# A state space scan: two VectorE operations a step on y alone, the chunks' own part summed by TensorE, the gate by one Silu

## The chip, the cores and the metric

The kernel runs on one core of a Trainium2 chip. The metric is the device time in microseconds (us) of one execution. Engines by the names of the profile: PE is TensorE, DVE is VectorE, ACT is ScalarE, POOL is GpSimd, SP is SyncE, which here only issues DMAs. PEld is TensorE's weight load, which overlaps its matmuls.

## The reference, cut to what matters

The program is a chain of two layers on one sequence of 2048 tokens with 128 channels: a state space mixer, a layer of experts, a causal attention, and then six blocks of windowed attention and feed-forward. The change is in the first of these, the state space mixer:

```python
A = relu(A_diag); dt = sigmoid(dt_p)
Bu = einsum('bth,phc->btpc', x, B_param)          # 128 states p, real and imaginary c
S = 1.0 / (1.0 + dt * dt * A)
m11, m12, m21, m22 = S, -dt * A * S, dt * S, S
f1, f2 = dt * S, dt * dt * S
def step(carry, bu):                              # 2048 steps
    z, y = carry
    z1 = c(m11) * z + c(m12) * y + c(f1) * bu
    y1 = c(m21) * z + c(m22) * y + c(f2) * bu
    return (z1, y1), y1
o = einsum(ys[..., 0], C_param[..., 0]) - einsum(ys[..., 1], C_param[..., 1]) + x * D
g = hidden @ Wg.T
o = o * rsqrt(mean(o * o) + EPS) * norm_weight * (g * sigmoid(g))
return o @ Wo.T
```

Here x is the normed input times Wi. From the two equations y alone obeys y[t] = 2 S y[t-1] - S y[t-2] + dt dt S bu[t], a recurrence of second order with no z in it. (The first equation gives dt z1 = y1 - y.)

## The kernel before, in words

The state lies with its 128 states p on the partitions. The 2048 steps are cut into 128 chunks of CL = 16 steps; the chunks lie side by side in the free dimension, so that one operation advances all of them, real and imaginary part, by one step: 128 partitions by 2 x 128 elements. The work of the front part has four stages.

- **Inputs** (ssm_step, ssm_inputs, lines 213 to 289): the step's coefficients; then for each of four groups of 512 tokens the layer norm ("ln_st", "ln_r", "ln_h", "ln_pt", "hT"; "ln_r" is a power on POOL), x by Wi ("px", kept as xsT), the two inputs Bu ("pb") scaled by dt S into f1 (laid out step, part, chunk), ACT for the real and DVE for the imaginary part, and the gate's product ("pg"). ACT makes Sigmoid of "pg" into sg and copies "pg" into the gate (a view of x3T); POOL multiplies the two.
- **Scan** (ssm_scan, lines 291 to 335), all on DVE: first the chunks' own recurrence, three operations a step (t from y, z from z and t, y from z), with ys and f1 as views of the tile kT; then the states at the chunks' ends go through seven doubling rounds of four operations each (the log scan, in zy, a view of hT3), with powers of the step's 2x2 matrix that POOL makes beside it (ssm_powers); then, for each of the 16 steps, two operations add what the state carried into the chunk contributes. The result yo is in token order.
- **Output** (ssm_out, lines 337 to 372): for each group "po" sums y by C and x by D on PE, DVE multiplies by the gate ("ou"), ACT makes the squares' sums ("osq"), PE transposes ("pu"), POOL makes the inverse root ("or_"), PE multiplies by Wo ("pr"), DVE adds to x.
- **Experts, keys and values, attention** follow ("own", "py", "pl", "pk", "pv").

Each engine runs its instructions in the order in which the program writes them (InOrder, line 56). From the output stage on that order comes from Merge (line 71): each group's work is a generator that yields a waiting time, and the pieces are written in the order of their due times. The times at which the groups begin stand in front (line 529): output of group 0 at 0, of 2 at 7, of 1 at 10, of 3 at 16; experts of group 0 at 9, of 1 at 22, of 2 at 41, of 3 at 57; keys and values from 43 on. These are numbers that set an order, not times. PSUM gives seven banks to all tiles of these stages.

Between the inputs and the scan, front puts on POOL: a memset of zy's left half, the powers, the products diag_d, ct, w_igo and bqk, two iotas, the split of two bias rows into three bf16 pieces (split_rows, with two DMAs on SP), and a memset of va (128 x 8192 elements), the attention's values. One tile pool ("s1") gives the scratch tiles; its tiles have two buffers where nothing else is said, zt among them.

Of the kernel before, what the change touches and what calls it, by code (L numbers as in the profile page):

```python
# [11 lines left out]
F32 = mybir.dt.float32  # L12
BF16 = mybir.dt.bfloat16
I32 = mybir.dt.int32
AF = mybir.ActivationFunctionType
ALU = mybir.AluOpType
# [3 lines left out]
P = 128  # L20
T = 2048
NT = T // P
G = 4
NG = NT // G
# [7 lines left out]
HD1 = P // HEADS1  # L32
# [13 lines left out]
CL = 16  # L46
NCH = T // CL
PAD = NCH // 2
# [45 lines left out]
class Kernel:  # L94
# [117 lines left out]

    def ssm_step(self, w):

        vec, dve = self.w1[1], self.dve
        am = w.tile([P, 1], F32, name="am")
        dve.tensor_scalar_max(am, vec[:, 0:1], 0.0)
        dt = w.tile([P, 1], F32, name="dt")
        self.act.activation(dt, vec[:, 1:2], AF.Sigmoid)
        dta = w.tile([P, 1], F32, name="dta")  # L220
        dve.tensor_tensor(dta, dt, am, ALU.mult)
        den = w.tile([P, 1], F32, name="den")
        dve.tensor_scalar(den, dta, dt, 1.0, ALU.mult, ALU.add)
        npow = int(math.log2(T // 2)) + 1
        pw = w.tile([P, npow, 4], F32, name="pw")
        dve.reciprocal(pw[:, 0, 0:1], den)
        dve.tensor_copy(pw[:, 0, 3:4], pw[:, 0, 0:1])
        dve.tensor_scalar(pw[:, 0, 1:2], dta, pw[:, 0, 0:1], -1.0, ALU.mult, ALU.mult)
        dve.tensor_scalar_mul(pw[:, 0, 2:3], dt, pw[:, 0, 0:1])
        return dt, pw  # L230

    def ssm_powers(self, w, pw):

# [21 lines left out]
            n, k = 2 * n, k + 1  # L255
        return rows

    def ssm_inputs(self, pool, psum, x, g, m21, f1, gate, xsT):

        w4, vec, bt, ct = self.w1  # L260
        cpg = GW // CL
        hT = pool.tile([P, GW], F32, name="hT", tag="t")
        yield from self.norm_transposed(pool, psum, x, g, hT)
        px = psum.tile([P, GW], F32, name="px", tag="b")
        self.pe.matmul(px, lhsT=w4[:, 0, :], rhs=hT, start=True, stop=True)
        xs_g = xsT[:, g * GW : (g + 1) * GW]
        self.dve.tensor_copy(xs_g, px)
        yield 3.0
        for c in range(2):
            pb = psum.tile([P, GW], F32, name="pb", tag="b")  # L270
            self.pe.matmul(pb, lhsT=bt[:, c, :], rhs=xs_g, start=True, stop=True)
            fg = f1[:, :, c, g * cpg : (g + 1) * cpg].rearrange("p l k -> p k l")
            pb = pb.rearrange("p (k l) -> p k l", l=CL)
            if c == 0:
                self.act.activation(fg, pb, AF.Copy, scale=m21)
            else:
                self.dve.tensor_scalar_mul(fg, pb, m21)
        yield 14.0
        pg = psum.tile([P, G, P], F32, name="pg", tag="b")
        for j in range(G):  # L280
            self.pe.matmul(
                pg[:, j, :], lhsT=hT[:, j * P : (j + 1) * P], rhs=w4[:, 1, :], start=True, stop=True
            )
        yield 3.0
        sg = pool.tile([P, G, P], F32, name="sg", tag="t")
        self.act.activation(sg, pg, AF.Sigmoid)
        gg = gate[:, g * G : (g + 1) * G, :]
        self.act.copy(gg, pg)
        self.gps.tensor_tensor(gg, gg, sg, ALU.mult)

    def ssm_scan(self, pool, dt, pw, rows, f1, ys, zy, yo):

        dve = self.dve
        s_, m12 = pw[:, 0, 0:1], pw[:, 0, 1:2]

        zp, yp = zy[:, 0:2], zy[:, 2:4]
        z = f1[:, 0]
        dve.tensor_scalar_mul(ys[:, 0], z, dt)
        for l in range(1, CL):
            t = pool.tile([P, 2, NCH], F32, name="zt")  # L300
            dve.scalar_tensor_tensor(t, ys[:, l - 1], m12, f1[:, l], ALU.mult, ALU.add)
            zn = pool.tile([P, 2, NCH], F32, name="zn") if l < CL - 1 else zp[:, 0, :, PAD:]
            dve.scalar_tensor_tensor(zn, z, s_, t, ALU.mult, ALU.add)
            dve.scalar_tensor_tensor(ys[:, l], zn, dt, ys[:, l - 1], ALU.mult, ALU.add)
            z = zn
        dve.tensor_copy(yp[:, 0, :, PAD:], ys[:, CL - 1])

        cur, step, k = 0, 1, int(math.log2(CL))
        while step < NCH:
            zc, yc, zn, yn = zp[:, cur], yp[:, cur], zp[:, 1 - cur], yp[:, 1 - cur]  # L310
            lo, hi = PAD - step, PAD + NCH - step
            ts = []
            for row, old in enumerate((zc, yc)):
                ts.append(pool.tile([P, 2, NCH], F32, name="zt"))
                dve.scalar_tensor_tensor(
                    ts[row], zc[:, :, lo:hi], pw[:, k, 2 * row : 2 * row + 1], old[:, :, PAD:],
                    ALU.mult, ALU.add,
                )
            for row, new in enumerate((zn, yn)):
                dve.scalar_tensor_tensor(  # L320
                    new[:, :, PAD:], yc[:, :, lo:hi], pw[:, k, 2 * row + 1 : 2 * row + 2], ts[row],
                    ALU.mult, ALU.add,
                )
            cur, step, k = 1 - cur, 2 * step, k + 1
        cz = zp[:, cur, :, PAD - 1 : PAD - 1 + NCH]
        cy = yp[:, cur, :, PAD - 1 : PAD - 1 + NCH]
        for l in range(CL):
            t = pool.tile([P, 2, NCH], F32, name="zt")
            dve.scalar_tensor_tensor(
                t, cz, rows[:, 0, l : l + 1], ys[:, l], ALU.mult, ALU.add  # L330
            )
            dve.scalar_tensor_tensor(
                yo.rearrange("p c (k l) -> p c k l", l=CL)[:, :, :, l], cy, rows[:, 1, l : l + 1], t,
                ALU.mult, ALU.add,
            )

    def ssm_out(self, pool, psum, x, g, gate, xsT, yo):

        w4, ct, diag_d = self.w1[0], self.w1[3], self.diag_d
        po = psum.tile([P, G, P], F32, name="po", tag="b")  # L340
        for j in range(G):
            cols = bass.ts(g * G + j, P)
            self.pe.matmul(po[:, j, :], lhsT=yo[:, 0, cols], rhs=ct[:, 0, :], start=True, stop=False)
            self.pe.matmul(po[:, j, :], lhsT=yo[:, 1, cols], rhs=ct[:, 1, :], start=False, stop=False)
            self.pe.matmul(po[:, j, :], lhsT=xsT[:, cols], rhs=diag_d, start=False, stop=True)
        yield 3.2
        u = pool.tile([P, G, P], F32, name="ou", tag="t")
        self.dve.tensor_tensor(u, po, gate[:, g * G : (g + 1) * G, :], ALU.mult)
        sq = pool.tile([P, G, P], F32, name="osq", tag="t")
# [126 lines left out]
    def front(self, ctx, merge, psum, kvpool, x, hT3, kT, va, xsT):  # L476


        nc, tc, gps = self.nc, self.tc, self.gps
# [13 lines left out]
        gate = self.x3T.rearrange("p (n c) -> p n c", c=P)  # L493
# [5 lines left out]
        zy = hT3[:, 0 : 8 * (PAD + NCH)].rearrange("p (a c k) -> p a c k", c=2, k=PAD + NCH)  # L499
        half = CL * 2 * NCH  # L500
        kf = kT.rearrange("p n t -> p (n t)")
        f1 = kf[:, 0:half].rearrange("p (l c k) -> p l c k", c=2, k=NCH)
        yo = kf[:, 0:half].rearrange("p (c t) -> p c t", c=2)
        ys = kf[:, half:].rearrange("p (l c k) -> p l c k", c=2, k=NCH)

        dt, pw = self.ssm_step(self.w1pool)
        first = Merge()
        for g in range(NG):
            first.add(2.5 * g, self.ssm_inputs(pool, psum, x, g, pw[:, 0, 2:3], f1, gate, xsT))
        first.run()  # L510
        gps.memset(zy[:, :, :, 0:PAD], 0.0)
        rows = self.ssm_powers(self.w1pool, pw)
        w4, vec, bt, ct = self.w1
        gps.tensor_scalar_mul(self.diag_d, self.ident, vec[:, 2:3])
        gps.tensor_scalar_mul(ct[:, 1, :], ct[:, 1, :], -1.0)
        gps.tensor_scalar_mul(w4[:, 2, :], w4[:, 2, :], vec[:, 3:4])
        gps.tensor_scalar_mul(bqk[:, 0, :], bqk[:, 0, :], HD1 ** -0.5)
        gps.iota(
# [3 lines left out]
            self.e_col, pattern=[[0, 1]], base=0, channel_multiplier=1, allow_small_or_imprecise_dtypes=True  # L522
        )
        self.split_rows()
        gps.memset(va, 0.0)
        gps.memset(va[:, :, :, HD1], 1.0)
        self.ssm_scan(pool, dt, pw, rows, f1, ys, zy, yo)

        begin = [(0, 9, 43, 51), (10, 22, 58, 66), (7, 41, 74, 87), (16, 57, 91, 111)]
        wait = []  # L530
        for g, (a, b, c, d) in enumerate(begin):
            wait.append(merge.add(a, self.ssm_out(pool, psum, x, g, gate, xsT, yo)))
            wait.append(merge.add(b, self.experts(pool, psum, x, g)))
            merge.add(c, self.keys_values(kvpool, psum, x, g, hT3, kT, va))
            merge.add(d, self.keys(psum, g, hT3, kT, range(1, NGRP)))
# [914 lines left out]
```

## Time and profile before

| what | us |
|---|---|
| three runs | 2554.53, 2558.29, 2561.1 (median 2558.29) |
| the profiled execution: its own time | 2556.16 |
| its span | 2554.1 |
| inputs, first instruction to the first scan operation | 0 to 36.3 |
| chunks' recurrence on DVE | 36.3 to 63.7 |
| log scan on DVE | 63.7 to 76.4 |
| carried part on DVE | 76.4 to 92.8 |
| first "po" matmul | 92.9 |
| first "ou" on DVE | 98.1 |

In the rows that follow, a group names the tile it writes and those it reads. Nearly every instruction shows line 66, the helper that records it, so that one goes by the tiles. Several tiles show the name of the memory they are views of: f1, ys and yo appear as kT, zy as hT, the gate as x3T. Durations overlap where an engine starts an instruction while the last one still writes: the time from start to start is then what counts.

### The profile page before, as it was taken

How to read it: one execution, taken by the hardware profiler on the slowest of the kernel's cores; microseconds unless marked ns; L12 is line 12 of the kernel's file. 1: busy time of each engine (PE TensorE's matmuls, PEld its weight loads, DVE VectorE, ACT ScalarE, POOL GpSimd, SP SyncE). 2: the span in 40 equal slices, each digit the busy share in tenths (PEclk: the TensorE clock that was granted, in tenths of full speed). 3: DMA queues.
4: the chain of work that ended last, by engine and by line, in shares of the span. 5: the costliest groups of instructions: out<-in, count | busy, mean ns of one | idle time of the engine just before them, and what ended most of it. 6: DMA issues, size and time to landing. Idle time of an engine off the chain costs nothing.

```text
span 2554.1 us, 87595 instructions
## 1 busy us (share of the span) xinstructions
PE 2416.1 (95%) x38248; PEld 1431.5 (56%) x38248; DVE 1860.4 (73%) x2548; ACT 1712.5 (67%) x3204; POOL 1490.5 (58%) x1011
## 2 busy tenths in 40 slices
PE   3498999999999799999999999999999999999997
PEld 1473333343334466666666666666666666666665
DVE  6775665467654477888788878887878788888884
ACT  1122455644556377888788878887888888888884
POOL 4310000010000588888888888788888878888880
PEclk8797999999999889999999999999999999999999
DMA  2000000000000322233222422233323332222221
GB/s 78 1 1 1 1 1 1 1 1 1 1 1 1 87 71 69 65 93 83 60 72 67 104 61 73 69 89 73 75 66 86 77 74 67 65 61 66 64 67 41
DMA packets 100155, 130.12 MB, mean 51 GB/s; under 512 B 26552, under 2 KB 47680, under 8 KB 99776
## 3 DMA queue, kind: packets, MB, share of 16 engines
q1 hardware_dynamic: 99196, 124.07, 19.6%
q8 instruction: 303, 4.96, 0.8%
q14 instruction: 76, 0.62, 0.1%
q10 hardware_dynamic: 580, 0.46, 0.1%
HBM read 23.50 MB, written 1.05 MB: 10 GB/s over the span
## 4 chain that ended last, share of the span: by engine, by line
PE 90%; issue 4%; DVE 2%; ACT 2%; POOL 1%; DMA 0%; POOLq 0%; ACTq 0%; DVEq 0%
PE sc L66 21%; PE ps L66 14%; PE po L66 9%; PE pt L66 7%; PE pv L66 7%; PE px L66 7%; PE av L66 6%; PE ph L66 5%; PE py L66 3%; PE ptp L66 3%; PE prb L66 1%; PE pvar L66 1%; PE pm L66 1%; ACT ex L66 1%; PE pq L66 1%
## 5 line engine op out<-in xcount | busy, mean ns | idle before, releaser
L66 POOL TENSOR_TENSOR rn<-ss,mhalf 128x32 f32<-128x32 f32 x96 | 524.3, 5462 | 8.0
L66 ACT ACTIVATE sm<-sm,mx,rn 128x64 f32<-128x64 f32 x1536 | 519.7, 429 | 3.3 <-POOL mx L66 2.8
L66 DVE TENSOR_REDUCE mx<-sc 128x1 f32<-128x512 f32 (+3 forms) x640 | 353.5, 604 | 225.1 <-PE sc L66 223.4
L66 ACT ACTIVATE ex<-sc 128x512 f32<-128x512 f32 (+3 forms) x640 | 306.0, 536 | 278.9 <-PE sc L66 278.0
L66 POOL TENSOR_TENSOR rot_a<-rot_a,rot_b 128x1024 f32<-128x1024 f32 x192 | 450.0, 2361 | 5.8 <-DVE rot_b L66 5.8
L66 PE MATMUL sc<-kT,qT 64*32 64x64 f32 (+2 forms) x13568 | 440.2, 258 | 8.9 <-ACT qT L66 7.8
L66 PE MATMUL ps<-wqkv,s 128*128 128x512 f32 x768 | 397.3, 621 | 1.6 <-DVE s L66 1.6
L66 POOL TENSOR_SCALAR_AFFINE_SELECT ex<-ex 128x512 f32<-128x512 f32 x64 | 40.8, 637 | 578.2 <-ACT ex L66 562.1
L66 PE MATMUL sc<-qT,kT 32*128 32x512 f32 (+3 forms) x1280 | 340.6, 583 | 4.0 <-DVE qT L66 2.1
L66 DVE TENSOR_TENSOR rot_a<-ps,tab 128x1024 f32<-128x1024 f32 x192 | 234.9, 1223 | 133.1 <-ACT sq L66 126.7
L66 PEld LDWEIGHTS sc<-kT,qT 64*32 64x32 f32 (+1 forms) x13568 | 218.5, 113 | 187.4 <-issue 108.5
L66 PEld LDWEIGHTS po<-pT,vw 64*64 64x64 f32 x12288 | 212.6, 137 | 186.5 <-issue 177.3
L66 ACT ACTIVATE sq<-ps 128x1024 f32<-128x1024 f32 x192 | 196.6, 1024 | 134.4 <-PE ps L66 96.4
L66 PE MATMUL po<-pT,vw 64*64 64x32 f32 x12288 | 244.0, 223 | 4.2 <-ACT pT L66 4.2
L66 DVE TENSOR_TENSOR rot_b<-ps,tab 128x1024 f32<-128x1024 f32 x192 | 232.9, 1213 | 0.0
L66 DVE TENSOR_REDUCE ss<-sq 128x16 f32<-128x1024 f32 x192 | 224.6, 1211 | 1.1
L66 PE MATMUL pt<-ident,rot_a 128*128 128x128 f32 x1536 | 211.7, 282 | 12.0 <-POOL rot_a L66 11.9
L66 PEld LDWEIGHTS pt<-ident,rot_a 128*128 128x128 f32 x1536 | 171.5, 143 | 46.5 <-issue 22.9
L66 PE MATMUL pv<-wqkv,s 128*128 128x512 f32 x384 | 191.6, 622 | 0.0
L66 PE MATMUL px<-oT,wo 64*128 64x128 f32 x3072 | 185.9, 276 | 0.8 <-DVE ot L66 0.8
L66 POOL TENSOR_TENSOR rot_a<-rot_a,rn 128x1024 f32<-128x1024 f32 x96 | 182.8, 1904 | 0.1
L66 PEld LDWEIGHTS px<-oT,wo 64*128 64x128 f32 x3072 | 176.7, 189 | 9.0 <-issue 4.5
(214 smaller groups left out, 3469.6 us busy)
## 6 DMA issues: line engine op xcount, KB each, us to landing
vw<-vt SPq DMA_DIRECT2D x1524, 64.0 KB
wqkv<-in_L_ffn_Wqkv SPq DMA_DIRECT2D x18, 512.0 KB
wo<-in_L_ffn_Wo SPq DMA_DIRECT2D x24, 256.0 KB
w<-in_L_ffn_W SPq DMA_DIRECT2D x6, 341.0 KB
x<-in_L_attn_hidden_states SPq DMA_DIRECT2D x4, 256.0 KB
out<-ot SPq DMA_DIRECT2D x4, 256.0 KB
rot<-in_rot SPq DMA_DIRECT2D x1, 960.0 KB
w<-in_L_ffn_W SPq DMA_DIRECT2D x12, 64.0 KB
```

The costliest lines, as they stand in the source:

```text
L66: return self._tc.keep_in_program_order(call(*args, **kw))
```

## The change

- ssm_step makes four coefficients: dt dt S, dt dt A, 2 S and -S, and a step matrix for the scaled state (dt z, y), whose entries are S, -dt dt A S, S and S.
- ssm_inputs scales the inputs by dt dt S and writes them into ys. The gate is one Silu of "pg" on ACT.
- ssm_chunks makes the chunks' recurrence on y alone, in place, with two DVE operations a step: minus S times y two back, and 2 S times y one back. ACT copies each step's y into yt, which is in token order. At the end dt z is the difference of the last two y.
- ssm_carry has the log scan as before. In the last 16 steps ACT scales the carried first state into t, and DVE adds the carried second state and writes u, the carried part alone, in token order; u is a view of va.
- ssm_out_own: PE sums, for all four groups, xsT by diag_d and yt by C into "po", before the carry is written; ssm_out then adds u by C to the same banks. The order of POOL's work is changed: diag_d and ct stand before zy's memset and the powers. The memset of va, whose memory u now uses, becomes a job of the merge, due at 20.0.

```diff
@@ -212,22 +212,25 @@
 
     def ssm_step(self, w):
 
+
         vec, dve = self.w1[1], self.dve
         am = w.tile([P, 1], F32, name="am")
         dve.tensor_scalar_max(am, vec[:, 0:1], 0.0)
         dt = w.tile([P, 1], F32, name="dt")
         self.act.activation(dt, vec[:, 1:2], AF.Sigmoid)
-        dta = w.tile([P, 1], F32, name="dta")
-        dve.tensor_tensor(dta, dt, am, ALU.mult)
-        den = w.tile([P, 1], F32, name="den")
-        dve.tensor_scalar(den, dta, dt, 1.0, ALU.mult, ALU.add)
+        co = w.tile([P, 4], F32, name="co")
+        dve.tensor_tensor(co[:, 0:1], dt, dt, ALU.mult)
+        dve.tensor_tensor(co[:, 1:2], co[:, 0:1], am, ALU.mult)
         npow = int(math.log2(T // 2)) + 1
         pw = w.tile([P, npow, 4], F32, name="pw")
-        dve.reciprocal(pw[:, 0, 0:1], den)
-        dve.tensor_copy(pw[:, 0, 3:4], pw[:, 0, 0:1])
-        dve.tensor_scalar(pw[:, 0, 1:2], dta, pw[:, 0, 0:1], -1.0, ALU.mult, ALU.mult)
-        dve.tensor_scalar_mul(pw[:, 0, 2:3], dt, pw[:, 0, 0:1])
-        return dt, pw
+        dve.tensor_scalar_add(pw[:, 0, 2:3], co[:, 1:2], 1.0)
+        dve.reciprocal(pw[:, 0, 0:1], pw[:, 0, 2:3])
+        dve.tensor_scalar(pw[:, 0, 1:2], co[:, 1:2], pw[:, 0, 0:1], -1.0, ALU.mult, ALU.mult)
+        dve.tensor_copy(pw[:, 0, 2:4], pw[:, 0, 0:1].to_broadcast([P, 2]))
+        dve.tensor_tensor(co[:, 0:1], co[:, 0:1], pw[:, 0, 0:1], ALU.mult)
+        dve.tensor_scalar_mul(co[:, 2:3], pw[:, 0, 0:1], 2.0)
+        dve.tensor_scalar_mul(co[:, 3:4], pw[:, 0, 0:1], -1.0)
+        return co, pw
 
     def ssm_powers(self, w, pw):
 
@@ -255,7 +258,7 @@
             n, k = 2 * n, k + 1
         return rows
 
-    def ssm_inputs(self, pool, psum, x, g, m21, f1, gate, xsT):
+    def ssm_inputs(self, pool, psum, x, g, into, f1, gate, xsT):
 
         w4, vec, bt, ct = self.w1
         cpg = GW // CL
@@ -272,9 +275,9 @@
             fg = f1[:, :, c, g * cpg : (g + 1) * cpg].rearrange("p l k -> p k l")
             pb = pb.rearrange("p (k l) -> p k l", l=CL)
             if c == 0:
-                self.act.activation(fg, pb, AF.Copy, scale=m21)
+                self.act.activation(fg, pb, AF.Copy, scale=into)
             else:
-                self.dve.tensor_scalar_mul(fg, pb, m21)
+                self.dve.tensor_scalar_mul(fg, pb, into)
         yield 14.0
         pg = psum.tile([P, G, P], F32, name="pg", tag="b")
         for j in range(G):
@@ -282,28 +285,25 @@
                 pg[:, j, :], lhsT=hT[:, j * P : (j + 1) * P], rhs=w4[:, 1, :], start=True, stop=True
             )
         yield 3.0
-        sg = pool.tile([P, G, P], F32, name="sg", tag="t")
-        self.act.activation(sg, pg, AF.Sigmoid)
-        gg = gate[:, g * G : (g + 1) * G, :]
-        self.act.copy(gg, pg)
-        self.gps.tensor_tensor(gg, gg, sg, ALU.mult)
-
-    def ssm_scan(self, pool, dt, pw, rows, f1, ys, zy, yo):
+        self.act.activation(gate[:, g * G : (g + 1) * G, :], pg, AF.Silu)
+
+    def ssm_chunks(self, co, ys, zy, yt):
+
 
         dve = self.dve
-        s_, m12 = pw[:, 0, 0:1], pw[:, 0, 1:2]
-
+        self.act.copy(yt[:, :, :, 0], ys[:, 0])
+        for l in range(1, CL):
+            if l > 1:
+                dve.scalar_tensor_tensor(ys[:, l], ys[:, l - 2], co[:, 3:4], ys[:, l], ALU.mult, ALU.add)
+            dve.scalar_tensor_tensor(ys[:, l], ys[:, l - 1], co[:, 2:3], ys[:, l], ALU.mult, ALU.add)
+            self.act.copy(yt[:, :, :, l], ys[:, l])
+        dve.tensor_tensor(zy[:, 0, :, PAD:], ys[:, CL - 1], ys[:, CL - 2], ALU.subtract)
+        dve.tensor_copy(zy[:, 2, :, PAD:], ys[:, CL - 1])
+
+    def ssm_carry(self, pool, pw, rows, zy, u):
+
+        dve = self.dve
         zp, yp = zy[:, 0:2], zy[:, 2:4]
-        z = f1[:, 0]
-        dve.tensor_scalar_mul(ys[:, 0], z, dt)
-        for l in range(1, CL):
-            t = pool.tile([P, 2, NCH], F32, name="zt")
-            dve.scalar_tensor_tensor(t, ys[:, l - 1], m12, f1[:, l], ALU.mult, ALU.add)
-            zn = pool.tile([P, 2, NCH], F32, name="zn") if l < CL - 1 else zp[:, 0, :, PAD:]
-            dve.scalar_tensor_tensor(zn, z, s_, t, ALU.mult, ALU.add)
-            dve.scalar_tensor_tensor(ys[:, l], zn, dt, ys[:, l - 1], ALU.mult, ALU.add)
-            z = zn
-        dve.tensor_copy(yp[:, 0, :, PAD:], ys[:, CL - 1])
 
         cur, step, k = 0, 1, int(math.log2(CL))
         while step < NCH:
@@ -326,24 +326,28 @@
         cy = yp[:, cur, :, PAD - 1 : PAD - 1 + NCH]
         for l in range(CL):
             t = pool.tile([P, 2, NCH], F32, name="zt")
-            dve.scalar_tensor_tensor(
-                t, cz, rows[:, 0, l : l + 1], ys[:, l], ALU.mult, ALU.add
-            )
-            dve.scalar_tensor_tensor(
-                yo.rearrange("p c (k l) -> p c k l", l=CL)[:, :, :, l], cy, rows[:, 1, l : l + 1], t,
-                ALU.mult, ALU.add,
-            )
-
-    def ssm_out(self, pool, psum, x, g, gate, xsT, yo):
-
-        w4, ct, diag_d = self.w1[0], self.w1[3], self.diag_d
+            self.act.activation(t, cz, AF.Copy, scale=rows[:, 0, l : l + 1])
+            dve.scalar_tensor_tensor(u[:, :, :, l], cy, rows[:, 1, l : l + 1], t, ALU.mult, ALU.add)
+
+    def ssm_out_own(self, psum, g, xsT, yt):
+
         po = psum.tile([P, G, P], F32, name="po", tag="b")
         for j in range(G):
             cols = bass.ts(g * G + j, P)
-            self.pe.matmul(po[:, j, :], lhsT=yo[:, 0, cols], rhs=ct[:, 0, :], start=True, stop=False)
-            self.pe.matmul(po[:, j, :], lhsT=yo[:, 1, cols], rhs=ct[:, 1, :], start=False, stop=False)
-            self.pe.matmul(po[:, j, :], lhsT=xsT[:, cols], rhs=diag_d, start=False, stop=True)
-        yield 3.2
+            self.pe.matmul(po[:, j, :], lhsT=xsT[:, cols], rhs=self.diag_d, start=j == 0, stop=False)
+            for c in range(2):
+                states = yt[:, c].rearrange("p k l -> p (k l)")[:, cols]
+                self.pe.matmul(po[:, j, :], lhsT=states, rhs=self.w1[3][:, c, :], start=False, stop=False)
+        return po
+
+    def ssm_out(self, pool, psum, x, g, gate, po, u):
+
+        w4 = self.w1[0]
+        for j in range(G):
+            for c in range(2):
+                states = u[:, c].rearrange("p k l -> p (k l)")[:, bass.ts(g * G + j, P)]
+                self.pe.matmul(po[:, j, :], lhsT=states, rhs=self.w1[3][:, c, :], start=False, stop=j + c == G)
+        yield 2.4
         u = pool.tile([P, G, P], F32, name="ou", tag="t")
         self.dve.tensor_tensor(u, po, gate[:, g * G : (g + 1) * G, :], ALU.mult)
         sq = pool.tile([P, G, P], F32, name="osq", tag="t")
@@ -499,20 +503,20 @@
         zy = hT3[:, 0 : 8 * (PAD + NCH)].rearrange("p (a c k) -> p a c k", c=2, k=PAD + NCH)
         half = CL * 2 * NCH
         kf = kT.rearrange("p n t -> p (n t)")
-        f1 = kf[:, 0:half].rearrange("p (l c k) -> p l c k", c=2, k=NCH)
-        yo = kf[:, 0:half].rearrange("p (c t) -> p c t", c=2)
-        ys = kf[:, half:].rearrange("p (l c k) -> p l c k", c=2, k=NCH)
-
-        dt, pw = self.ssm_step(self.w1pool)
+        ys = kf[:, 0:half].rearrange("p (l c k) -> p l c k", c=2, k=NCH)
+        yt = kf[:, half:].rearrange("p (c k l) -> p c k l", c=2, l=CL)
+        u = va.rearrange("p n h s -> p (n h s)")[:, 0:half].rearrange("p (c k l) -> p c k l", c=2, l=CL)
+
+        co, pw = self.ssm_step(self.w1pool)
         first = Merge()
         for g in range(NG):
-            first.add(2.5 * g, self.ssm_inputs(pool, psum, x, g, pw[:, 0, 2:3], f1, gate, xsT))
+            first.add(2.5 * g, self.ssm_inputs(pool, psum, x, g, co[:, 0:1], ys, gate, xsT))
         first.run()
-        gps.memset(zy[:, :, :, 0:PAD], 0.0)
-        rows = self.ssm_powers(self.w1pool, pw)
         w4, vec, bt, ct = self.w1
         gps.tensor_scalar_mul(self.diag_d, self.ident, vec[:, 2:3])
         gps.tensor_scalar_mul(ct[:, 1, :], ct[:, 1, :], -1.0)
+        gps.memset(zy[:, :, :, 0:PAD], 0.0)
+        rows = self.ssm_powers(self.w1pool, pw)
         gps.tensor_scalar_mul(w4[:, 2, :], w4[:, 2, :], vec[:, 3:4])
         gps.tensor_scalar_mul(bqk[:, 0, :], bqk[:, 0, :], HD1 ** -0.5)
         gps.iota(
@@ -522,14 +526,20 @@
             self.e_col, pattern=[[0, 1]], base=0, channel_multiplier=1, allow_small_or_imprecise_dtypes=True
         )
         self.split_rows()
-        gps.memset(va, 0.0)
-        gps.memset(va[:, :, :, HD1], 1.0)
-        self.ssm_scan(pool, dt, pw, rows, f1, ys, zy, yo)
+        self.ssm_chunks(co, ys, zy, yt)
+        own = [self.ssm_out_own(psum, g, xsT, yt) for g in range(NG)]
+        self.ssm_carry(pool, pw, rows, zy, u)
 
         begin = [(0, 9, 43, 51), (10, 22, 58, 66), (7, 41, 74, 87), (16, 57, 91, 111)]
+        def ones():
+            gps.memset(va, 0.0)
+            gps.memset(va[:, :, :, HD1], 1.0)
+            yield 0.0
+
         wait = []
+        merge.add(20.0, ones())
         for g, (a, b, c, d) in enumerate(begin):
-            wait.append(merge.add(a, self.ssm_out(pool, psum, x, g, gate, xsT, yo)))
+            wait.append(merge.add(a, self.ssm_out(pool, psum, x, g, gate, own[g], u)))
             wait.append(merge.add(b, self.experts(pool, psum, x, g)))
             merge.add(c, self.keys_values(kvpool, psum, x, g, hT3, kT, va))
             merge.add(d, self.keys(psum, g, hT3, kT, range(1, NGRP)))
```

## The prediction

> **What bounds the kernel now.** I read the page's shares and its chain first, then the chain in order of time over the first 190 us, then busy time by stretch, then the instructions in order of time, tile by tile. On the page TensorE is the engine that ends last:
>
> ```profile
> PE 2416.1 (95%) x38248; PEld 1431.5 (56%) x38248; DVE 1860.4 (73%) x2548; ACT 1712.5 (67%) x3204; POOL 1490.5 (58%) x1011
> PE 90%; issue 4%; DVE 2%; ACT 2%; POOL 1%; DMA 0%; POOLq 0%; ACTq 0%; DVEq 0%
> ```
>
> But that is an average over stages. In the state space scan TensorE does nothing. First the chain there, then busy time by stretch (us of PE, PEld, DVE, ACT, POOL, then TensorE's granted clock):
>
> ```profile
> 39.97 52.95 issue
> 92.92 5.12 PE po L66 x24
> ...
> 36.00:64.00 28.00, 2.59 (x24) 2.40 (x22) 26.25 (x49) 3.96 (x8) 25.73 (x72) 0.62 0.00 0
> 64.00:76.40 12.40, 0.00 (x0) 0.00 (x0) 12.40 (x30) 0.00 (x0) 11.70 (x23) 0.50 0.00 0
> 76.40:93.00 16.60, 0.08 (x1) 0.11 (x1) 15.51 (x33) 0.00 (x0) 7.23 (x6) 0.50 0.00 0
> ```
>
> VectorE alone sets the time from 36.3 to 92.8 us, with ACT idle in the last two stretches. Everything behind it waits for the first "po" matmul, so what the scan loses or gains goes to the end: from 187 us on no wait for a DMA appears among the waits of the compute engines, and TensorE is busy 302 of 313 us in the stretch 187 to 500. The scan's rows (ns minimum/median/maximum):
>
> ```profile
> L66 DVE SCALAR_TENSOR_TENSOR zt<-hT,rows,kT x16: 460/465/472, 76.4 to 91.7; 128x256 f32<-128x256 f32 x16
> L66 DVE SCALAR_TENSOR_TENSOR kT<-hT,rows,zt x16: 646/652/659, 76.9 to 92.2; 128x256 f32<-128x256 f32 x16
> L66 DVE SCALAR_TENSOR_TENSOR zt<-kT,pw x15: 483/485/1365, 36.7 to 62.2; 128x256 f32<-128x256 f32 x15
> L66 POOL TENSOR_TENSOR x3T<-x3T,sg x4: 1273/1441/1446, 37.1 to 41.1; 128x512 f32<-128x512 f32 x4
> ```
>
> The median is 0.485 us, the maximum 1.365: the slow ones fall where POOL multiplies the gate. In order of time (start, us):
>
> ```profile
> 37.18 1.48 DVE L66 SCALAR_TENSOR_TENSOR zn<-kT,pw,zt 128x256 f32<-128x256 f32 x1
> 49.15 0.48 DVE L66 SCALAR_TENSOR_TENSOR kT<-zn,dt,kT 128x256 f32<-128x256 f32 x1
> 64.73 0.87 DVE L66 SCALAR_TENSOR_TENSOR hT<-hT,pw,zt 128x256 f32<-128x256 f32 x2
> 74.52 7.51 POOL L66 MEMSET va<- 128x8192 f32 x2
> 119.34 1.01 POOL L66 TENSOR_TENSOR or__869<-oss,mhalf 128x4 f32<-128x4 f32 x1 [5.82 <-DVE oss L66]
> 121.67 1.01 POOL L66 TENSOR_TENSOR ln_r<-ln_var,mhalf 128x4 f32<-128x4 f32 x1 [1.33 <-DVE ln_var L66]
> 124.33 1.11 DVE L66 TENSOR_SCALAR ln_h<-x,ln_mv,ln_r 128x128 f32<-128x128 f32 x4
> ```
>
> Two paces are to be seen: an operation that needs the one just before it starts 0.52 us after it (49.15, 49.67, ...); in the log scan, where each needs the one two back, a pair takes 0.79 us, so 0.395 each.
>
> **The change, part by part.** The sum is against this execution's own 2556.16 us (span 2554.1 and 2.1 around it), 2.1 us under the median of the three runs, 2558.29.
>
> *Front (ssm_step, POOL's order).* After dt there are nine small VectorE operations instead of six, 0.12 us apart where independent and 0.2 to 0.24 where dependent: +0.5 us, straight on the chain, since "ln_st" starts when they end. POOL's diag_d (1.14) and ct (0.73) and the 25 us of powers now start at about 20 us, when POOL has its last "ln_r" behind it, and no longer at 42.5. They then stand beside the front's "ln_h" instead of the scan. Beside the scan the tiny power operations cost nothing (0.52 held) and diag_d 0.04 us; beside "ln_h" the trace has nothing, so 0 to 2 us; I take 0.5, nearer to the scan's rows. Together -1.0.
>
> *Gate.* ACT's Sigmoid and Copy of 0.6 us each become one Silu a group, and POOL's four products go. A Silu that isn't in the loaded table costs one more load, 1.28 us by the row at 112 us. ACT ends its f1 writes at 35.3 and the gate's last matmul ends at 38.6, so the load is covered; if it were not, it delays only the gate, which is needed 35 us later, and the copies below. The Silus end near 39.7, where the old pair ended at 40.0. What is gained is VectorE's: four steps of 1.43 instead of 0.52, counted in the next part.
>
> *Chunk recurrence.* Before, 36.27 to 63.73: 27.5 us (46 operations, the slow four among them). After, 29 operations. The subtraction of y two back needs nothing that has just been made, so a pair costs 0.395 + 0.52 = 0.915: 14 x 0.915 + 0.52 = 13.3 us. POOL's tail (w_igo, bqk, the rows' split) cost the log scan 1.35 us at 68 to 75 us (pairs of 0.83 to 1.34 instead of 0.79); at the new start it falls at the end of the chunk part, so I move 1.35 here: 14.65, a gain of 12.8. The log scan loses it: 12.42 becomes 28 x 0.395 = 11.06, +1.35. Joining costs one more operation of 0.4 us (nearest row 0.395 of a pair): -0.4.
>
> [...] The paces 0.52 and 0.395 of this trace differ by just the dependence, so I go by the row.
>
> ACT's sixteen copies into chunk order write with a step of 16 elements. The nearest rows are the f1 writes, 1.13 for 512 elements with a step, and a plain copy, 0.28 at 128 and 0.59 at 512: between 0.4 and 1.13 us, I take 0.6. VectorE needs 0.9 a step, so ACT catches up and ends 0.6 behind; the copies have until 63 us, 1.45 us each, before they hold the carry.
>
> *PE sums the chunks' own part.* 48 matmuls (two passes each, 0.21 us a pass at clock 0.5, 0.11 at full) start near 52 and take about 13 us: beside the log scan and the carry, which end near 73. Cover gone, they would hold "po" by what remains. Four PSUM banks of seven are held, three left for "pu" and "pr"; the merged order frees one before each further need.
>
> *Carry.* Before, 16 steps of two VectorE operations, 76.36 to 92.82: 16.5 us. After, VectorE keeps the strided one, 0.50 us from start to start, 0.65 to its end. ACT scales; between the per-partition-scale row at 128 elements (ye, 0.375) and the bias row at 512 (0.70) lies 0.48 at 256. zt has two buffers, so two steps go round as 0.65 + 0.03 + 0.48 + 0.03 = 1.19, 0.6 a step (0.03 is the handover seen between ou and osq at 98.8). 0.25 lead + 15 x 0.6 + 0.65 = 9.9: +6.55. Ends: 0.50 a step (8.4) and 0.7 if VectorE must see its own strided write end (11.4).
>
> *ssm_out.* Four groups lose a third of their matmuls, 24 passes to 16. The first, at clock 0.5: 5.1 to 3.4, +1.7. Groups 2 and 1 stand in a row behind it (102.4 to 108.7 in the chain): two thirds of that would give 2.1, VectorE's norm statistics up to 105.4 hold part, I take 1.0 (0 to 2.1). +2.7.
>
> *ones (the va memset, 7.5 us).* Before it lay beside the scan. Now it is due at 20.0 in the merge; group 3's product comes at 16 + 2.4 + 0.9 + 0.7, a hair before, so POOL runs or (group 3), memset, then "ln_r" of group 1's experts and all that follows. By the rows above: or ends 120.35, the memset then ends 127.95, "ln_r" 129.0, and "ln_h" starts at 129.1 instead of 124.33. "ln_h" stands in VectorE's order ahead of four "own", for which TensorE waits. 4.8, less 0.4 because TensorE had a backlog to 125.9: -4.4. Ends: 0, if another path were later there, and 7.5. SP's two row transfers wait for POOL's pieces 58 us before; they only move earlier.
>
> Sum: -1.0 + 12.8 + 1.35 - 0.4 + 6.55 + 2.7 - 4.4 = 17.6 us; 2556.2 - 17.6 = 2538.6, said as 2539.
>
> **Rivals.** (a) *One pace for all*: each operation of the recurrence starts 0.52 us after the one before, dependent or not, as all of the old recurrence's do: 29 x 0.52 = 15.1 us, 1.8 more, 2540.4. Against: the log scan's pairs, the same operation at 0.395. [...] (b) *The carry runs in single file*: ACT and VectorE hand over without overlap, 1.19 a step: 0.25 + 16 x 1.19 = 19.3, 9.4 us more than taken, 2548. For: every step now crosses engines twice, which the trace nowhere shows at this rate; against: two buffers. (c) *Given back to the clock*: TensorE ran at 0.85 and 0.92 in 93 to 150 us; after a scan without matmuls it starts at 0.5, and now with a third less work to stay busy, and with a pause at the memset. Work that goes at half instead of about 0.9 takes 0.8 of its time more, so 22 us of matmul time kept slow would eat the 17.6: no change, about 2556. Against: in 93 to 98 us the first full stretch of work sufficed for full speed. (d) *Slower, ACT becomes the bound*: the stepped copies stand ahead of the scales in ACT's order. At 1.45 us each they begin to hold the carry; to end 7.7 us above the old time they must take (23 + 25)/16 = 3.0 us each: 2564 and up. Against: the nearest row is 1.13 for twice the elements.
>
> **How the numbers follow.** Forecast 0.60, own range 2530 to 2546 (from the ends: carry -1.5/+1.5, memset +4.4/-3.1, front +0.5/-1.5, own part of the clock and ssm_out +-1.5, runs +-3); (a) 0.10; (b) 0.12; (c) 0.09; (d) 0.06; more than the forecast's range 0.03. The range must leave out no more than 2 in 10: (c), (d) and the 0.03 are left out, so it reaches over (b), 2530 to 2551. A measurement of this kernel tells about 0.3%, 7.7 us, from no change: faster 0.60 + 0.10 + 0.12 + 0.03 = 0.85, same 0.09, slower 0.06.
>
> **What would show it.** 29 operations of 0.48 us with pairs of 0.915 and none of 1.4; one more table load near 36 us; ACT copies of about 0.6 us; matmuls "po" near 52 to 65 us; a carry step of 0.6 us, ACT and VectorE in turn; the first "ou" near 77 us; a POOL memset of 7 us with VectorE idle ahead of "ln_h", releaser POOL, for 4 to 5 us; and from there on the old order some 18 us earlier. The prediction is wrong if copies or scales on ACT take over 1.4 us, if the carry goes at 1.2 a step, or if TensorE's clock stays at 0.5 past the first two groups.

## The result, and the profile after

The changed kernel takes 2535.49 us in the median of six runs (2534.49 to 2550.19); the kernel before, in six runs of the same comparison, 2557.66. The ratio is 0.9927, with a 95% interval of 0.9901 to 0.9953: faster by 0.5 to 1.0%. The forecast was 2539, in a range from 2530 to 2551. The profiled execution took 2534.71 us (before: 2556.16), so 21.4 us less, where the sum gave 17.6.

The page of the changed kernel, shares and chain:

```profile
PE 2423.0 (96%) x38312; PEld 1441.2 (57%) x38312; DVE 1844.1 (73%) x2519; ACT 1728.4 (68%) x3233; POOL 1471.4 (58%) x1007
PE 90%; DVE 4%; ACT 3%; POOL 1%; issue 1%; DMA 0%; ACTq 0%; DVEq 0%; POOLq 0%
```

DVE has 29 instructions fewer and ACT 29 more. Of the 4% of "issue" in the chain before, 53 us (2%) were the scan; in their place the chain now names the operations of DVE and ACT. Busy time by stretch, as before (us of PE, PEld, DVE, ACT, POOL, then TensorE's clock):

```profile
36.00:52.00 16.00, 3.53 (x32) 3.33 (x30) 15.36 (x33) 12.73 (x22) 5.01 (x14) 0.75 0.00 0
52.00:63.00 11.00, 10.87 (x74) 10.87 (x75) 11.00 (x29) 0.22 (x2) 0.00 (x0) 0.75 0.01 1
63.00:73.60 10.60, 2.44 (x22) 2.25 (x21) 9.21 (x17) 7.50 (x16) 0.00 (x0) 0.72 0.00 1
```

TensorE now works through the whole log scan, ACT through recurrence and carry; the scan ends at 73.6 us instead of 92.8. The operations of recurrence and carry, and ACT's copies and scales (the first and last two by tile, the third from the groups of ACT between 36 and 75 us):

```profile
L66 DVE SCALAR_TENSOR_TENSOR kT<-kT,co x29: 479/485/890, 37.0 to 50.9; 128x256 f32<-128x256 f32 x29
...
L66 ACT COPY kT<-kT 128x256 f32<-128x256 f32 x16 | 9.3, 632 | 2.9 <-DVE kT L66 2.9
...
L66 ACT ACTIVATE zt<-hT,rows x16: 494/509/510, 62.9 to 72.4; 128x256 f32<-128x256 f32 x16
L66 DVE SCALAR_TENSOR_TENSOR va<-hT,rows,zt x16: 629/646/658, 63.4 to 72.9; 128x256 f32<-128x256 f32 x16
```

And the place of the moved memset, in order of time:

```profile
96.61 1.01 POOL L66 TENSOR_TENSOR or__855<-oss,mhalf 128x4 f32<-128x4 f32 x1 [5.61 <-DVE oss L66]
97.57 7.51 POOL L66 MEMSET va<- 128x8192 f32 x2
...
98.70 5.82 DVE L66 TENSOR_SCALAR ln_var<-ln_mv 128x4 f32<-128x4 f32 x1
...
104.96 1.01 POOL L66 TENSOR_TENSOR ln_r<-ln_var,mhalf 128x4 f32<-128x4 f32 x1
106.00 1.11 DVE L66 TENSOR_SCALAR ln_h<-x,ln_mv,ln_r 128x128 f32<-128x128 f32 x4 [1.48 <-POOL ln_r L66]
113.17 0.69 DVE L66 TENSOR_REDUCE mx<-pl 128x4 f32<-128x512 f32 x1 [2.94 <-PE pl L66]
```

The line to stop at is ln_var: an operation on 4 elements a partition, 0.17 us everywhere else in this execution, lasts 5.82 us and ends at 104.52, when POOL's large memset does (104.49). Four x and three own, which started behind it at their usual distances, end with it at 104.52. The forecast had VectorE waiting too, but at ln_h and because of POOL's order.

### The profile page after: what moved, and what is told of

Its sections match the earlier page's. It is cut to its first block, busy times and chain, and to the rows that moved or that the text cites. A ratio compares the mean times of both kernels' runs of the same rounds, so it can differ in the third digit from the quotient of the medians.

```text
span 2533.0 us, 87720 instructions
## 1 busy us (share of the span) xinstructions
PE 2423.0 (96%) x38312; PEld 1441.2 (57%) x38312; DVE 1844.1 (73%) x2519; ACT 1728.4 (68%) x3233; POOL 1471.4 (58%) x1007
## 4 chain that ended last, share of the span: by engine, by line
PE 90%; DVE 4%; ACT 3%; POOL 1%; issue 1%; DMA 0%; ACTq 0%; DVEq 0%; POOLq 0%
PE sc L66 21%; PE ps L66 14%; PE po L66 9%; PE pt L66 7%; PE pv L66 7%; PE px L66 7%; PE av L66 6%; PE ph L66 5%; PE py L66 4%; PE ptp L66 3%; PE prb L66 1%; PE pvar L66 1%; PE pm L66 1%; ACT ex L66 1%; DVE kT L66 1%
## 5 line engine op out<-in xcount | busy, mean ns | idle before, releaser
L66 PEld LDWEIGHTS sc<-kT,qT 64*32 64x32 f32 (+1 forms) x13568 | 219.5, 113 | 188.6 <-issue 108.7
```

The source lines that it names most:

```text
L66: return self._tc.keep_in_program_order(call(*args, **kw))
```

## Where the time went, stretch by stretch

"mx<-pl" of the second group's experts is the landmark behind all that the change touches: 129.59 us before, 113.17 after.

| stretch | before | after | gain | forecast |
|---|---|---|---|---|
| to the first operation of the scan | 36.27 | 36.98 | -0.7 | -1.0 |
| chunk recurrence | 27.46 | 14.46 | +13.0 | +12.8 |
| joining | 0.21 | 0.54 | -0.3 | -0.4 |
| log scan | 12.42 | 11.09 | +1.3 | +1.35 |
| carry, to the end of the last operation | 16.46 | 10.51 | +5.95 | +6.55 |
| from there to the end of group 3's or_ | 27.53 | 24.04 | +3.5 | +2.7 |
| from there to the second mx<-pl | 9.24 | 15.55 | -6.3 | -4.4 |
| sum | 129.59 | 113.17 | +16.4 | +17.6 |

The last stretch has two parts. To the start of ln_h it lost 4.4 us (from the end of or_: 3.99 before, 8.38 after). From ln_h to mx it lost another 1.9 (5.26, 7.17). There the chain of the changed kernel shows TensorE:

```profile
98.90 5.62 DVE x L66 x4
104.62 4.88 PE py L66 x24
109.94 1.79 PE py L66 x16
```

The three own that ended only at 104.52 left 24 "py" matmuls in a row, and TensorE's granted clock was 0.50 from 98.5 to 108.7 us. "ln_pt" stands behind them in TensorE's order and started at 109.34, although the first ln_h was done at 106.35.

The other 5.0 us of this pair of executions lie behind the landmark, in code that the change doesn't touch; they are treated at the end of the experiments.

## The experiments

The theories were: the memset costs its full length at VectorE (against: only POOL's order counts, or TensorE's clock), the carry goes at the round trip of two buffers (against: VectorE's own strided write), the recurrence gains by dependence as well as by count (against: one pace for all), the gate slowed the scan through POOL (against: fresh operands), and the own part is really hidden. The first masked exp of the attention (188.37 us in the changed kernel, 204.97 before) serves as a second landmark.

### The memset later

```diff
-        merge.add(20.0, ones())
+        merge.add(33.0, ones())
```

> The va memset becomes due at 33.0 in the merge, behind the first group's POOL addition, instead of 20.0. Theory (the memset is what holds VectorE at ln_var and ln_h): no VectorE operation of over 2 us is left near the end of the output stage; the experts' second maximum (mx<-pl, second of its kind) starts near 107 instead of 113.2 us (6.3 us was lost there against the kernel before, measured from or_ of group 3), and the memset costs about 1 us at the next ln_var, so the first masked exp of the attention (ex on POOL) starts near 183 instead of 188.4; time about 5 us less than the changed kernel, give or take the clock's 5 us. Rival (the loss there is TensorE at half clock, not the memset): the second maximum stays at 112 to 113.

Of this run only the 0.17 us of its ln_var is used: the profiled execution took 3441 us (the other three 2534.55 to 2539.5), for the reason that the next expectation names. The same kernel once more:

> The same kernel as e1_late, whose profiled execution had TensorE at a granted clock of 0.63 throughout. As expected there: ln_var 0.17 us, the second mx<-pl near 107 us instead of 113.2, the first masked exp of the attention near 183 instead of 188.4.

```profile
98.46 0.17 DVE L66 TENSOR_SCALAR ln_var<-ln_mv 128x4 f32<-128x4 f32 x1
107.61 0.69 DVE L66 TENSOR_REDUCE mx<-pl 128x4 f32<-128x512 f32 x1 [2.68 <-PE pl L66]
113.45 7.53 POOL L66 MEMSET va<- 128x8192 f32 x2
```

ln_var is short again, the landmark comes 5.6 us earlier and the first masked exp at 181.48, 6.9 earlier. Behind the first POOL addition the memset costs nothing that shows. It is the memset, then, that starts the loss. The clock is not excluded as a part of it: in 97 to 108 us it was 0.57 in the changed kernel and 0.84 here, so it came back with the edit, and how the 5.6 us divide between the wait and the slower clock behind it is not shown. The time, 2534.96 us (ratio 0.9911, 0.9889 to 0.9933), does not show the 7 us; see the end of this section.

### The memset behind ln_r

```diff
-        merge.add(20.0, ones())
+        merge.add(22.5, ones())
```

> The va memset becomes due at 22.5, just behind ln_r of the second group's experts, nothing else. Theory A (VectorE only waits for ln_r, which stands in POOL's order behind the memset): all of the loss comes back, the second mx<-pl starts near 107 us. Theory B (while POOL's memset runs, VectorE's operations with one input in SBUF and the output in SBUF stand still): ln_var passes, but ln_h, which now meets the running memset, lasts until the memset ends near 107 us, and the second mx<-pl starts at 112 to 114, about as in the changed kernel.

In order of time:

```profile
99.36 1.01 POOL L66 TENSOR_TENSOR ln_r<-ln_var,mhalf 128x4 f32<-128x4 f32 x1 [1.32 <-DVE ln_var L66]
100.32 7.55 POOL L66 MEMSET va<- 128x8192 f32 x2
...
100.69 1.13 DVE L66 SCALAR_TENSOR_TENSOR x<-pr,or__855,x 128x128 f32<-128x128 f32 x4 [1.40 <-PE pr L66]
101.73 1.88 DVE L66 SCALAR_TENSOR_TENSOR own<-pi,hT 128x512 f32<-128x512 f32 x3
...
103.52 4.50 DVE L66 TENSOR_SCALAR ln_h<-x,ln_mv,ln_r 128x128 f32<-128x128 f32 x4
```

Theory B. Nothing waits for POOL's order any more, ln_r is done at 100.4, and still the four ln_h, 1.11 us elsewhere, last 4.50: the first two end when the memset's large part does, at 107.3. The operations between, with one input from PSUM, run at their usual pace beside the same memset (1.13 for four, 1.88 for three). The landmark stands at 112.16 us, 1.0 less than in the changed kernel; the time is 2539.41 us. Before the change the scan's operations with two inputs took 0.46 to 0.66 us beside that memset, but 1.36 to 1.48 beside the gate's product; why the one holds them and the other doesn't is not shown. Not every operation from SBUF to SBUF is stopped: in the changed kernel the norm's statistics (BATCH_NORM_STATS2 and its AGGREGATE) kept their 0.26 and 0.18 us beside the memset, from 97.69 to 98.66 us.

### Half of the memset

u lies in the first half of va, so the second half can be set early:

```diff
+        gps.memset(va[:, NT // 2 :], 0.0)
         self.ssm_chunks(co, ys, zy, yt)
...
-            gps.memset(va, 0.0)
+            gps.memset(va[:, 0 : NT // 2], 0.0)
```

> The changed kernel; the half of va that u does not use is set to zero beside the recurrence, the job at 20.0 sets only the other half. Theory (VectorE's operations from SBUF to SBUF stand still for as long as POOL's memset runs): ln_var lasts about 2.4 us instead of 5.82, the second mx<-pl starts 3.4 us earlier, near 109.8. If only POOL's order counted, the same 3.4 us would show at ln_h and ln_var would last 0.17.

```profile
97.38 4.11 POOL L66 MEMSET va<- 128x4096 f32 x2
...
98.50 2.41 DVE L66 TENSOR_SCALAR ln_var<-ln_mv 128x4 f32<-128x4 f32 x1
109.25 0.69 DVE L66 TENSOR_REDUCE mx<-pl 128x4 f32<-128x512 f32 x1 [2.59 <-PE pl L66]
```

2.41 us, as worked out: ln_var ends at 100.91, and the memset's large part at about 100.9 (97.38 + 4.11, less the 0.58 that the small one behind it adds in the changed kernel). Beside the early half (39.89 to 43.39 us) the recurrence's operations took 0.47 to 0.49 us, as without it; the slow ones, up to 0.89, lie ahead of it, beside the rows' split. 2527.59 us, ratio 0.9888 (0.9866 to 0.9910). When this kernel was run again (below), ln_var lasted 2.41 us once more, but the landmark stood at 107.62, as early as without any memset there (107.61). TensorE's clock in 97 to 108 us was 0.72 here and 0.84 in both of those. So what a wait at ln_var costs at the landmark is not its length alone.

### The carry with four buffers

```diff
-            t = pool.tile([P, 2, NCH], F32, name="zt")
+            t = pool.tile([P, 2, NCH], F32, name="zc", bufs=4)
```

> The carried part's scaled state gets a tile of its own with four buffers instead of two. Theory (the 0.643 us a step of the changed kernel is the round trip between ACT and VectorE over two buffers): a step falls to VectorE's own pace, 0.50 to 0.55 us, and the carry ends 1.5 to 2.3 us earlier, the first ou near 75.5 instead of 77.45. Rival (VectorE waits for its own strided write before the next one): 0.64 us a step as before.

```profile
63.50 7.84 DVE L66 SCALAR_TENSOR_TENSOR va<-hT,rows,zc 128x256 f32<-128x256 f32 x16 [0.29 <-ACT zc L66]
75.17 0.69 DVE L66 TENSOR_TENSOR ou<-po,x3T 128x512 f32<-128x512 f32 x1 [3.83 <-PE po L66]
```

The sixteen operations run as one group without a wait: 15 steps in 7.84 less the last 0.65, 0.48 us a step, where the changed kernel needs 0.63. The first ou is 2.3 us earlier. It was the round trip. At the second mx<-pl only 0.5 us of the gain is left (112.68 against 113.17). 2535.64 us, ratio 0.9912 (0.9893 to 0.9931).

### The recurrence's two operations exchanged

```diff
-            if l > 1:
-                dve.scalar_tensor_tensor(ys[:, l], ys[:, l - 2], co[:, 3:4], ys[:, l], ALU.mult, ALU.add)
             dve.scalar_tensor_tensor(ys[:, l], ys[:, l - 1], co[:, 2:3], ys[:, l], ALU.mult, ALU.add)
+            if l > 1:
+                dve.scalar_tensor_tensor(ys[:, l], ys[:, l - 2], co[:, 3:4], ys[:, l], ALU.mult, ALU.add)
```

> The changed kernel with the two operations of a recurrence step exchanged: first the product with y one back, then the one with y two back. The same 29 operations, but now each needs the one just before it. Theory (what spaces the operations is the dependence: 0.395 us behind an independent one, 0.52 behind its own source): all 29 go at 0.52, the pairs at 1.04 instead of 0.915, the recurrence lasts 14 x 0.125 = 1.75 us longer, 16.2 instead of 14.46 us. [...]

The group in order of time, then one line of the chain:

```profile
37.24 15.67 DVE L66 SCALAR_TENSOR_TENSOR kT<-kT,co 128x256 f32<-128x256 f32 x29
...
40.45 0.50 DVE kT L66
```

15.71 us to the next operation instead of 14.46. Where POOL is quiet the chain shows every operation 0.52 us after the one before; in the changed kernel pairs of 0.917. The first operations, beside POOL's row split, lose 0.6 us here and 1.1 there, which is why the difference is 1.25 and not 1.75. The same operations, only in another order: the dependence sets the pace. The changed kernel's trace shows where the time goes: an operation that reads its neighbour's output waits for VectorE's own semaphore and starts 0.035 us after that neighbour's end (at 41.754 us, the end being 41.719), one without such a wait 0.083 us before it (at 42.156, the end being 42.239). There every second operation has the wait; in the exchanged order all 28 behind the first read their neighbour's output. What the dependence would cost without the wait is not tried. The time is 2539.77 us, ratio 0.9938 (0.9905 to 0.9971).

### One part alone: the gate by Silu in the kernel before

```diff
-        sg = pool.tile([P, G, P], F32, name="sg", tag="t")
-        self.act.activation(sg, pg, AF.Sigmoid)
-        gg = gate[:, g * G : (g + 1) * G, :]
-        self.act.copy(gg, pg)
-        self.gps.tensor_tensor(gg, gg, sg, ALU.mult)
+        self.act.activation(gate[:, g * G : (g + 1) * G, :], pg, AF.Silu)
```

> The kernel before with one part of the change alone: the gate by one Silu on ACT, no product on POOL. Theory (the four slow operations at the start of the scan stand still because POOL reads and writes SBUF beside them): no scan operation over 0.5 us near 37 to 43 us, the chunk recurrence takes 23.8 instead of 27.5 us, and all behind it is 3.65 us earlier; the time falls by about 3.7 us, inside what the clock scatters. POOL's powers start at 21 instead of 42.5 us. Rival (they are slow for another reason, as their operands were just written by ACT): 27.5 us as before and no gain.

```profile
37.77 0.77 DVE L66 SCALAR_TENSOR_TENSOR kT<-zn,dt,kT 128x256 f32<-128x256 f32 x1
40.45 0.48 DVE L66 SCALAR_TENSOR_TENSOR zt<-kT,pw 128x256 f32<-128x256 f32 x1
60.88 0.29 DVE L66 COPY hT<-kT 128x256 f32<-128x256 f32 x1
```

The operations of 1.4 us are gone. The recurrence takes 24.8 us, not the 23.8 of the theory: POOL, freed, reaches its row split at 37 to 40 us and slows a few operations to 0.67 to 0.77. The log scan gets that back, 11.1 instead of 12.4 us. The first ou comes 4.1 us earlier, at 94.05. 2550.52 us, ratio 0.9973 (0.9956 to 0.9990).

### The own part not ahead

```diff
-        own = [self.ssm_out_own(psum, g, xsT, yt) for g in range(NG)]
...
+        po = self.ssm_out_own(psum, g, xsT, yt)
```

(the first line in front, the last at the head of ssm_out)

> The changed kernel with one part undone: TensorE sums the chunks' own part only behind the carry, in each group's own turn, 20 matmuls a group there instead of 8. Theory (the own part is covered by log scan and carry, and its absence behind the carry shortens ssm_out): the first ou starts 2.9 us later, 80.3 instead of 77.45 (22 passes at 0.21, then 18 at 0.11), and or_ of group 3 ends 4 to 7 us later than 97.6. Rival (ssm_out goes at VectorE's and ACT's pace, TensorE's matmuls matter only in the first group): about 3 us later there.

```profile
76.49 0.69 DVE L66 TENSOR_TENSOR ou<-po,x3T 128x512 f32<-128x512 f32 x1 [3.77 <-PE po L66]
...
86.24 0.69 DVE L66 TENSOR_TENSOR ou<-po,x3T 128x512 f32<-128x512 f32 x1 [2.76 <-PE po L66]
```

The first ou is not later: group 0's own part stands first in TensorE's order, so it still ran during the log scan, which I had overlooked. The other three groups' parts now lie behind the carry: VectorE waits 2.76, 1.37 and 1.77 us for "po" at the next three ou, and or_ of group 3 ends at 104.87 instead of 97.62, 7.2 us later, a little over the theory's 4 to 7. So the own part is covered, and TensorE's matmuls do set ssm_out's pace. The time is 2538.96 us, ratio 0.9931 (0.9913 to 0.9950).

### Which of it reaches the end

Three kernels were run again to see the scatter: the changed one, the one with the halved memset beside it, and one with all three edits (four buffers, half of the memset early, the other half at 33.0). The last has two runs here:

> The changed kernel once more, unaltered, beside the next run, to see how far executions of one kernel scatter behind the front part. Expected: recurrence 14.5 us, first masked exp of the attention at 187 to 189.5 us; from there to the end 2342 to 2356 us, by how often TensorE's clock drops; median 2534 to 2542.

> The kernel with half of the memset beside the recurrence, as e7_half, once more beside the changed kernel on one chip. Theory: the 5 us that the first masked exp gains against the changed kernel are in the time, 3 to 8 us less than the run beside it. Rival (the 8 us between the two medians so far were the clock's scatter): no difference between the medians of over 2 us.

> Three edits to the changed kernel: four buffers for the carried part's scaled state; the half of va that u does not use is set to zero beside the recurrence; the other half (about 3.5 us) is set at 33.0 in the merge, behind the first POOL addition. If the two causes found so far (round trip over two buffers, 2.1 us; the memset against VectorE, 6.3 us) are the ones and add up: carry step 0.49 us, first ou near 75.2, second mx<-pl near 105, first masked exp of the attention near 180 instead of 188.4, time about 2527 to 2531. If the memset is only moved to hurt elsewhere: first masked exp at 184 to 186.

> The kernel with three edits (e5_best) once more, in more rounds. Theory (the gain before the attention is carried through, and the clock scatters the rest): first masked exp of the attention at 179 to 183 us, time 2525 to 2540 with a median near 2531, ratio to the kernel before 0.988 to 0.991. Rival (what the front gains is always given back behind it): median 2536, as the changed kernel.

The first masked exp, and the time from there to the span's end, in one profiled execution each:

| kernel | first masked exp, us | from there to the end, us | granted clock |
|---|---|---|---|
| before | 204.97 | 2349.1 | 0.969 |
| changed | 188.37 | 2344.6 | 0.975 |
| changed, again | 188.17 | 2349.3 | 0.974 |
| own part not ahead | 193.31 | 2343.1 | 0.976 |
| half memset | 183.19 | 2341.9 | 0.979 |
| half memset, again | 181.47 | 2351.2 | 0.975 |
| all three edits | 181.85 | 2356.4 | 0.971 |
| all three edits, again | 179.99 | 2351.4 | 0.974 |

From that point all these kernels have the same work, and it takes between 2341.9 and 2356.4 us. That scatter is larger than what the first pair of profiles gained behind the landmark: in instruction order their gain is 16.6 us at the first masked exp, 25.8 at the seventh, 20.3 at the 37th, 18.4 at the 61st and 21.1 at the span's end. Among the changed kernels the longest rest goes with the lowest granted clock of the whole execution (0.971) and the shortest with the highest (0.979). The kernel before has a lower one, 0.969, with a rest in the middle, but there the clock was 0.5 from 43 us to behind the end of the scan. Counted behind the first masked exp alone, TensorE stood at half clock for 65 us where the rest took 2341.9, for 86 in the kernel before, and for 107 where it took 2356.4. That the clock is the cause is argued from this, not tried.

Run beside the changed kernel, the one with half of the memset took 2537.3 us against 2536.29, so the rival of that expectation stood: one set of six runs does not show a front that is 6.7 us shorter. Over all runs of each kernel the medians are 2535.9 us for the changed kernel (12 runs, 2531.6 to 2550.2), 2533.9 with half of the memset (10 runs, 2524.8 to 2542.8) and 2531.4 with all three edits (10 runs, 2525.0 to 2541.3; ratio in the second set of runs 0.9910, 0.9888 to 0.9933). The last is the best version found, by 4.5 us in the median, which these runs make likely rather than certain. Four buffers and a later memset also did not add up before the attention: with all three edits the second mx<-pl stood at 107.94 and 107.54 us where the later memset alone had 107.61, although the first ou was 2.3 to 2.8 us earlier. The lead is lost behind the first ou: the second one follows it 7.1 and 8.1 us later, where with the later memset alone it took 6.6. TensorE's clock in 75 to 85 us was 0.83 and 0.60 there, and 0.86 with the later memset alone; that this is the cause is not shown.

## Why the prediction was right, step by step

- **Chunk recurrence.** Right in size (14.65 forecast, 14.46 measured) and in its reason, the pairs of 0.915 (0.917 measured), which the exchanged order confirms. One detail was wrong without effect: POOL's tail was put at the end of the recurrence, from powers of 25 us. They took 13.8 us (21.8 to 35.6), because POOL's small operations took 0.34 us a pair beside the inputs, where they took 0.58 beside the scan; so the tail fell on the first steps, and cost 1.1 us there instead of 1.35. ACT's copies took 0.63 us (0.6 forecast), although the 0.28 us read as a plain copy at 128 elements belongs to the squares, osq.
- **Gate.** The table load stood where it was put (36.08, 1.28 us) and was covered; the 1.4 us operations went. Right.
- **Carry.** 9.9 forecast, 10.5 measured, by the round trip that was named; mis-sized by 0.03 us a step, since the scale took 0.51 instead of 0.48 and a handover 0.03 us in some steps and 0.10 in others, where 0.03 was taken; the lead was 0.38 instead of 0.25. Single file did not come.
- **ssm_out.** 2.7 forecast, 3.5 measured. Up to the first ou it gained 1.4 instead of 1.7, from there to or_ of group 3 2.0 instead of 1.0, the upper end of what was given for groups 2 and 1.
- **ones.** The term that was mis-sized: 4.4 forecast, 6.3 measured. That the memset would hold VectorE was right, the reason was only half: VectorE stopped already at ln_var, which needs nothing of POOL. Up to ln_h the loss was 4.4 us, near the 4.8 worked out from POOL's order. That order still stood, with ln_r behind the memset, so this number does not tell the two reasons apart; the run with the memset behind ln_r does. The 0.4 taken off for TensorE's backlog had the wrong sign: the three "own" that were to keep TensorE busy stopped too, and their matmuls, at half clock, cost 1.9 us more behind ln_h. That is a small piece of rival (c), which had named the pause at the memset.
- **Front.** -0.7 against -1.0; the bound of 2 us was not needed. The changed kernels of the table above reach the scan between 35.90 and 36.98 us with the same front, so the 0.7 itself is inside the scatter.
- **Total.** The sum, 17.6, and the measured 16.4 at the landmark lie close by errors of both signs, so the nearness is in part luck. The rest to 21.4 in the profiled pair, and the spread of the runs, belong to code behind it and were allowed for by 3 us either way; the profiles show 7.

## What to carry to other kernels

When an operation is moved to POOL's free time, look at which VectorE operations run beside it: here a memset was harmless beside operations with an input in PSUM (1.13 us for four x, 1.88 for three own) or with two inputs (0.46 to 0.66 us in the scan before), and stopped a short SBUF to SBUF tensor_scalar for as long as it still ran (ln_var 5.82 us instead of 0.17, four ln_h 4.50 instead of 1.11), and in the first case the four x and three own behind it on VectorE, up to 104.52 us. When a loop is split between two engines, work out the round trip over its buffers and not only each engine's pace; two more buffers gave 0.15 us a step here, though only 0.5 us of the 2.3 were left at the landmark. And compare the edit's own stretch up to a landmark just behind it, because code that did not change scattered by 14 us here, more than most single edits gain.

## What I had not expected of the hardware

- A VectorE operation of 0.17 us lasting 5.82 beside a POOL memset, with no semaphore between the two: ln_var's only wait is for VectorE's own.
- The same operation starting 0.395 or 0.52 us after its neighbour (0.402 or 0.515 in the changed kernel's recurrence), by whether it has to wait for that neighbour's end.
- POOL's small operations taking 0.34 us a pair beside the inputs and 0.58 beside the scan, while the scan beside them kept its 0.52 us from one operation to the next.
- The time behind the change varying from 2341.9 to 2356.4 us with the same instructions.
